# Values by seven products instead of eight, in turns with the keys

## The chip, the cores and the metric

The kernel runs on one core of a Trainium2 chip. The metric is the device time of one execution in microseconds; the time of a kernel is the median of several runs. All data are 32-bit floats.

## The reference

Sixteen batches of `x` (1024 nodes by 256 channels) go through two residual layers that share one 1024 x 1024 adjacency. The first layer forms queries by a graph product, keys and values by one weight matrix, and attends with four heads; the second is a two-step graph convolution. Cut to what matters here:

```python
c_adj = mean(x over channels)
A_s = symmetric likeness of c_adj[n], c_adj[m]
g = relu(einsum('bcn,bnm->bcm', x^T, adj * A_s) * para)     # queries
kv = x @ kv_w                                               # (B, N, 2C)
k, v = first C columns, last C columns, split into 4 heads of 64
attn = softmax(q k^T * scale)
x = layernorm(x + attn v)
h = relu(x @ w1_loop + adj @ (x @ w1_neigh) + b1)
h = relu(h @ w2_loop + adj @ (h @ w2_neigh) + b2)
x = layernorm(x + (x + h) * 0.5)
```

The change touches how `x @ kv_w` is computed and where one step of the softmax's denominators stands.

## The kernel before

One program handles the batches one after the other, with the order of every engine's work written out by hand (`manual_schedule`). In the loop over `b`, the attention of batch b is interleaved with the second layer of batches b-1 and b-2 and with the queries, keys and values of batch b+1.

**Attention** (`Attention`) runs over four units, a pair of heads by a half of the query nodes. `scores(u)` makes eight score tiles on TensorE (line 594), each exponentiated by ScalarE (L597) and summed by VectorE (L601, L603), then transposed (L605) and reduced (L607) into partial denominators. `outputs(u)` multiplies by the values (L614), and VectorE transposes the result (L618). `add(u)` folds the partial denominators with one small matmul (L626, tile `den_ps`), takes reciprocals (L630), multiplies (L632), adds to the residual (L634) and reduces (L635). Between units stand `gap0`, `gap1` and `gap2`; `gap0` holds the convolution's inner product (L712, tile `t_ps`) and then `att.add(0)`, `gap1` the joined adjacency products.

**Keys and values** (`KeysValues`) are made after the queries of the same batch. The transposed input `xT` and the key half of the weights are each cut into 2 x 2 blocks, and seven products of block sums replace eight (a Winograd form of Strassen's scheme): `sums` makes four combinations of `xT` on VectorE (L384 to L387), and four combinations of weight blocks are made once at the start on GpSimd (`sum_key_weights`, L135 to L138), stored in device memory and loaded again for each batch (`load`, L392). In `run`, products are accumulated onto PSUM that ScalarE has copied away in between (L411, L415, L420, L422 into `ksnap`), and the last additions are done by VectorE (L418, L426), GpSimd (L427) and, as a copy, ScalarE (L429). The values take the plain form: four groups (`value_group`) of four 128 x 128 by 128 x 256 matmuls each (L360), copied by ScalarE (L362). Groups stand between the key products.

In `run`, `between` is called before the first key addition and `later` before the last products. In the steady state they are `norm.variance` (a fold of squares, `sum_ps`, L250, then L324 on VectorE and a power on GpSimd, L326) and `q.scale` (L569 on VectorE, L570 on ScalarE). After `run` come `norm.scale` (L331) and `norm.spread` (transposes L219 and stores). The queries' end (L555 to L563) stands before `run`.

PSUM has three double banks (`big_psum`, tag "big") and two single ones (`bank_psum`). Row tiles of 128 x 1024 come from one pool of 25.

Of the kernel before, what the change touches and what calls it, by code (L numbers as in the profile page):

```python
# [10 lines left out]
F32 = mybir.dt.float32  # L11
# [7 lines left out]
def kernel(  # L19
# [31 lines left out]
    nc = tc.nc  # L51

    B, N, C = x.shape
    P = 128
    NT = N // P
    NC = C // P
# [3 lines left out]
    FB = 512  # L60
    NJ = N // FB
    TJ = FB // P
    EPS = 1e-5
# [19 lines left out]
    dram = ctx.enter_context(tc.tile_pool(name="dram", bufs=2, space=bass.MemoryType.DRAM))  # L83
# [15 lines left out]
    def row_tile(name):  # L99
        return work.tile([P, N], F32, tag="row", name=name, bufs=ROWS)  # L100
# [15 lines left out]
    for t0 in range(0, NT, 2):  # L116
        nc.sync.dma_start(out=x_first[:, t0:t0 + 2, :],
                          in_=x[0, t0 * P:(t0 + 2) * P, :].rearrange("(t p) c -> p t c", p=P))
    kvw_sb = const.tile([P, NC, 2 * C], F32, name="kvw_sb")
# [6 lines left out]
    b2_sb = const.tile([P, C], F32, name="b2_sb")  # L126


    key_sums = dram.tile([P, 4 * P], F32, tag="key_sums", name="key_sums", bufs=1)

    def sum_key_weights():
        a11, a21, a12, a22 = (kvw_sb[:, cc, ts(kb, P)] for cc in range(NC) for kb in range(NC))
        t = row_tile("key_sums")
        s1, s2, s3, s4 = (t[:, ts(n, P)] for n in range(4))
        nc.gpsimd.tensor_add(s1, a21, a22)  # L135
        nc.gpsimd.tensor_sub(s2, s1, a11)
        nc.gpsimd.tensor_sub(s3, a11, a21)
        nc.gpsimd.tensor_sub(s4, a12, s2)  # L138
        nc.sync.dma_start(out=key_sums, in_=t[:, 0:4 * P])

    def load_weights():
        nc.sync.dma_start(out=w1l_sb, in_=w1_loop.rearrange("(cc p) f -> p cc f", p=P))
# [101 lines left out]
        nc.scalar.copy(c_row, pc)  # L244
        return c_row

    def fold_sums(part, name):

        pm = bank_psum(f"{name}_ps")
        nc.tensor.matmul(pm[:, 0:NB], fold.rearrange("p a k -> p (a k)"), part[:, 0, :], start=True, stop=True)  # L250
        return pm[:, 0:NB]

# [45 lines left out]
    class BlockedNorm:  # L298
# [22 lines left out]

        def variance(self):
            self.rstd = small.tile([P, NB], F32, tag="rstd1", name=f"rstd1_{self.name}", bufs=2)
            nc.vector.tensor_scalar(self.rstd, fold_sums(self.part, f"sum2_{self.name}"), 1.0 / C, EPS,  # L324
                                    op0=ALU.mult, op1=ALU.add)
            nc.gpsimd.tensor_tensor(self.rstd, self.rstd, neg_half, ALU.pow)  # L326

# [27 lines left out]
    def value_group(b, v, xT, g, copy):  # L355
        per = FB // C
        pv = bank_psum(f"v_ps_{b}_{g}")
        for i in range(per):
            for cc in range(NC):
                nc.tensor.matmul(pv[:, ts(i, C)], xT[:, cc, ts(g * per + i, P)], kvw_sb[:, cc, C:2 * C],  # L360
                                 start=(cc == 0), stop=(cc == NC - 1))
        copy(v[:, g * per:(g + 1) * per, :], pv.rearrange("p (i c) -> p i c", c=C))  # L362
# [7 lines left out]
    class KeysValues:  # L370
# [17 lines left out]
            self.w = {1: w11, 2: w21, 3: w22, 4: t4, 5: t1, 6: t2, 7: t3}  # L388

        def load(self):  # L390
            t = row_tile(f"key_sums_{self.b}")
            nc.sync.dma_start(out=t[:, 0:4 * P], in_=key_sums)  # L392
            a11, a21, a12, a22 = (kvw_sb[:, cc, ts(kb, P)] for cc in range(NC) for kb in range(NC))
            self.a = {1: a11, 2: a12, 3: t[:, ts(3, P)], 4: a22, 5: t[:, ts(0, P)], 6: t[:, ts(1, P)], 7: t[:, ts(2, P)]}

        def run(self, between=lambda: None, later=lambda: None):
            b, xT = self.b, self.xT
            kT = work.tile([P, NC, N], F32, tag="kT", name=f"kT_{b}")
            v = work.tile([P, NT, C], F32, tag="v", name=f"v_{b}")
            first, third, second = (half_psum(f"k_ps_{b}_{i}") for i in range(3))  # L400
            s12, s34 = (row_tile(f"ksnap_{b}_{k}") for k in range(2))
            p1, u1, u3, p7 = s12[:, 0:FB], s12[:, FB:N], s34[:, 0:FB], s34[:, FB:N]

            def product(n, dst, again=False):
                nc.tensor.matmul(dst, self.a[n], self.w[n], start=not again, stop=True, skip_group_check=again)

            def group(g):
                value_group(b, v, xT, g, nc.scalar.copy)

            product(1, first)  # L410
            nc.scalar.copy(p1, first)  # L411
            product(2, third)
            group(0)
            product(6, first, again=True)
            nc.scalar.copy(u1, first)  # L415
            group(1)
            between()
            nc.vector.tensor_add(kT[:, 0, 0:FB], p1, third)  # L418
            product(5, first, again=True)
            nc.scalar.copy(u3, first)  # L420
            product(7, second)
            nc.scalar.copy(p7, second)  # L422
            group(2)
            later()
            product(4, second, again=True)
            nc.vector.tensor_add(kT[:, 1, 0:FB], u1, second)  # L426
            nc.gpsimd.tensor_add(kT[:, 1, FB:N], u3, p7)  # L427
            product(3, first, again=True)
            nc.scalar.copy(kT[:, 0, FB:N], first)  # L429
            group(3)  # L430
            return kT, v

    class Queries:
# [49 lines left out]
    class FastQueries(Queries):  # L483
# [16 lines left out]
        def block(self, i, j):  # L500
            return self.xb[:, j * TJ:(j + 1) * TJ, ts(i, P)]
# [70 lines left out]
    class Attention:  # L572
# [47 lines left out]
        def add(self, u):  # L620

            b, (pair, j) = self.b, UNITS[u]
            half = FB // S
            pd = bank_psum(f"den_ps_{b}_{u}")
            den = pd[:, 0:2 * half]
            nc.tensor.matmul(den, fold.rearrange("p a k -> p (a k)"), self.part.pop(u), start=True, stop=True)  # L626
            rden = self.rden[:, ts(u, half)]
            for s in range(2):
                rows = slice(s * HD, (s + 1) * HD)
                nc.vector.reciprocal(rden[rows, :], den[rows, ts(s, half)])  # L630
            o = by_node(self.o.pop(u))
            nc.vector.tensor_mul(o, o, rden.unsqueeze(2).to_broadcast([P, half, S]))  # L632
            dst = by_node(self.xB[pair][:, ts(j, FB)])
            nc.vector.tensor_add(dst, dst, o)  # L634
            nc.vector.tensor_reduce(self.sums[:, pair, ts(j, half)], dst, AX.X, ALU.add)  # L635
            if u == len(UNITS) - 1:
                join(self.sums)
                nc.vector.tensor_reduce(rden_min[:, b:b + 1], self.rden, AX.X, ALU.min)
                nc.vector.tensor_reduce(rden_max[:, b:b + 1], self.rden, AX.X, ALU.max)
# [293 lines left out]
    def run():  # L933
# [10 lines left out]
        xT, c_col = prepare_first(x_first)  # L944
        q = Queries(0, x_first)
        for t in range(NT):
            q.load(t)
        sum_key_weights()
        q.load_para()
        blocked = load_blocked(1, "1")  # L950
        tiles = {mt: adj_blocked(mt) for mt in (0, TJ, 1)}
# [6 lines left out]
        kT = keys(0, xT, first_weights)  # L958
        for t in (1, 2):
            q.likeness(t)  # L960
        v = values(0, xT, nc.vector.tensor_copy, 3)
# [29 lines left out]
        for b in range(B):  # L991
            more = b + 1 < B
            att = Attention(b, xB, qT, kT, v)
# [12 lines left out]
            def gap0():  # L1006
                row = means(q, xb, str(b + 1))
                c1.inner()
                att.add(0)
                if both:  # L1010
                    c2.load_x()
                    both.fetch(2, 3)
                    both.left(nc.gpsimd)
                row()
                ready["xT"] = channel_major(blocked, f"xT_{b + 1}")
# [34 lines left out]
            for u in range(len(UNITS)):  # L1050
                att.scores(u)
                if u == 1 and between:
                    kv = KeysValues(b + 1, ready["xT"])
                    kv.sums()
                if u == 3 and between:
                    for t in (2, TJ + 2, 3, TJ + 3):
                        q.load(t)
                    for t in (2, TJ + 2, 3, TJ + 3):
                        q.likeness(t)
                    q.right(1)  # L1060
                if u and (not between or u == 3 and not both):
# [167 lines left out]
```

## Time and profile before

| | |
|---|---|
| median of 3 runs | 2168.17 us (2167.69 to 2169.34) |
| profiled execution, whole time | 2168.41 us |
| its span, first to last instruction | 2166.5 us |
| mean granted TensorE clock | 0.998 |
| a value pass, v_ps, L360 | 512 passes, 120.9 us busy |
| a key product's pass, k_ps, L405 | 210 passes in all |
| inner product, t_ps, L712 | 512 passes, 61.3 us busy |
| load of the block sums, L392 | 256 KB, once for each of 15 batches |

Engines in the profile are PE (TensorE's matmuls), PEld (its weight loads), DVE (VectorE), ACT (ScalarE), POOL (GpSimd) and SP (the queue that issues the transfers). A group line gives line, engine, operation, tiles and shapes, then the count, the busy time, the mean length of one, and the idle time ahead of it with what ended it. A timeline line gives the start, the time covered, the engine and the merged instructions. An f32 matmul appears as two passes, each with its own weight load. Ends of matmuls are modelled and overlap the next start, so spacing is read from starts.

### The profile page before, as it was taken

How to read it: one execution, taken by the hardware profiler on the slowest of the kernel's cores; microseconds unless marked ns; L12 is line 12 of the kernel's file. 1: busy time of each engine (PE TensorE's matmuls, PEld its weight loads, DVE VectorE, ACT ScalarE, POOL GpSimd, SP SyncE). 2: the span in 40 equal slices, each digit the busy share in tenths (PEclk: the TensorE clock that was granted, in tenths of full speed). 3: DMA queues.
4: the chain of work that ended last, by engine and by line, in shares of the span. 5: the costliest groups of instructions: out<-in, count | busy, mean ns of one | idle time of the engine just before them, and what ended most of it. 6: DMA issues, size and time to landing. Idle time of an engine off the chain costs nothing.

```text
span 2166.5 us, 23100 instructions
## 1 busy us (share of the span) xinstructions
PE 2152.7 (99%) x8052; PEld 1024.6 (47%) x8052; DVE 1892.1 (87%) x2342; ACT 1033.5 (48%) x1359; POOL 368.5 (17%) x212
## 2 busy tenths in 40 slices
PE   9999999999999999999999999999999999999997
PEld 5344444444444444454545445454454444544354
DVE  5988988898998989998899888999989899898964
ACT  4745445545345554445443454445553445535412
POOL 1010130311303113030120302203022130211021
PEclk9999999999999999999999999999999999999999
DMA  9493664836557365573656537566374554744342
GB/s 229 121 139 117 144 153 105 144 126 119 154 122 160 107 121 156 127 168 89 115 171 121 158 88 116 171 122 156 97 117 160 122 156 115 122 148 82 118 136 99
DMA packets 611916, 286.49 MB, mean 132 GB/s; under 512 B 504784, under 2 KB 569168, under 8 KB 611792
## 3 DMA queue, kind: packets, MB, share of 16 engines
q1 hardware_dynamic: 611520, 284.41, 55.4%
q8 instruction: 65, 1.06, 0.2%
q14 instruction: 59, 0.48, 0.1%
q10 hardware_dynamic: 272, 0.52, 0.1%
HBM read 238.42 MB, written 46.46 MB: 131 GB/s over the span
## 4 chain that ended last, share of the span: by engine, by line


## 5 line engine op out<-in xcount | busy, mean ns | idle before, releaser
L597 ACT ACTIVATE pr<-s 128x1024 f32<-128x1024 f32 x512 | 476.1, 1054 | 176.1 <-PE s L594 176.1
L603 DVE TENSOR_TENSOR acc<-acc,pr 128x1024 f32<-128x1024 f32 x384 | 494.2, 1287 | 41.1 <-DVE acc L603 1.0
L594 PE MATMUL s<-qT,kT 64*128 64x512 f32 x2048 | 456.8, 596 | 0.0
L614 PE MATMUL av<-pr,v 128*64 128x512 f32 x2048 | 453.6, 595 | 0.0
L594 PEld LDWEIGHTS s<-qT,kT 64*128 64x128 f32 x2048 | 191.6, 186 | 234.9 <-ACT pr L597 111.3
L614 PEld LDWEIGHTS av<-pr,v 128*64 128x64 f32 x2048 | 141.3, 137 | 299.3 <-issue 284.9
L326 POOL TENSOR_TENSOR rstd<-rstd,neg_half 128x32 f32<-128x32 f32 x16 | 87.1, 5442 | 1113.1 <-DVE rstd L324 1113.1
L459 ACT ACTIVATE wg<-c_row,c_col 128x1024 f32<-128x1024 f32 x128 | 147.0, 1148 | 69.2 <-DVE accB L605 50.5
L465 DVE SCALAR_TENSOR_TENSOR wg<-wg,adj 128x1024 f32<-128x1024 f32 x128 | 150.0, 1210 | 12.8 <-ACT wg L460 11.9
L892 PE MATMUL hu_ps<-adj,R 128*128 128x512 f32 x360 | 158.3, 596 | 0.0
L460 ACT ACTIVATE wg<-wg 128x1024 f32<-128x1024 f32 x128 | 135.4, 1058 | 4.1
L314 ACT ACTIVATE sq<-xB_a 128x1024 f32<-128x1024 f32 x32 | 33.8, 1057 | 197.0 <-DVE xB_a L309 195.7
L360 PE MATMUL v_ps<-kvw_sb,xT 128*128 128x256 f32 x512 | 120.9, 379 | 0.1
L546 PE MATMUL g_ps<-wg,S 128*128 128x512 f32 x224 | 116.7, 603 | 0.0
L360 PEld LDWEIGHTS v_ps<-kvw_sb,xT 128*128 128x128 f32 x512 | 97.2, 190 | 40.1 <-issue 22.5
L546 PE MATMUL g_ps<-T,S 128*128 128x512 f32 x224 | 114.4, 592 | 0.0
L546 PE MATMUL g_ps<-wg,x 128*128 128x512 f32 x224 | 109.0, 599 | 0.0
L892 PE MATMUL hu_ps<-adjT,t 128*128 128x512 f32 x240 | 105.7, 592 | 0.0
L892 PEld LDWEIGHTS hu_ps<-adj,R 128*128 128x128 f32 x360 | 67.3, 190 | 78.9 <-issue 76.0
L601 DVE TENSOR_TENSOR acc<-pr,pr 128x1024 f32<-128x1024 f32 x64 | 76.8, 1201 | 20.5 <-ACT pr L597 20.5
L605 DVE STREAM_TRANSPOSE accB<-acc 128x1024 f32<-128x1024 f32 x64 | 79.7, 1245 | 3.3
L908 ACT COPY snap<-hu_ps 128x512 f32<-128x512 f32 x15 | 8.8, 585 | 150.3 <-PE hu_ps L892 146.2
(189 smaller groups left out, 2923.0 us busy)
## 6 DMA issues: line engine op xcount, KB each, us to landing
adj<-in_adj_dram SPq DMA_DIRECT2D x128, 512.0 KB, 4.7
adj<-adjT SPq DMA_DIRECT2D x120, 512.0 KB, 10.2
para<-in_L_gnn_para_dram SPq DMA_DIRECT2D x32, 512.0 KB, 3.4
xB_a<-in_x_dram SPq DMA_DIRECT2D x128, 128.0 KB, 4.3
x1d<-xB_a SPq DMA_DIRECT2D x128, 128.0 KB, 3.4
x<-x1d SPq DMA_DIRECT2D x16, 1024.0 KB, 16.5
xB<-in_x_dram SPq DMA_DIRECT2D x120, 128.0 KB, 4.3
x<-in_x_dram SPq DMA_DIRECT2D x15, 1024.0 KB, 7.9
```

What stands on the lines that cost most here:

```text
L326: nc.gpsimd.tensor_tensor(self.rstd, self.rstd, neg_half, ALU.pow)
L360: nc.tensor.matmul(pv[:, ts(i, C)], xT[:, cc, ts(g * per + i, P)], kvw_sb[:, cc, C:2 * C], start=(cc == 0), stop=(cc == NC - 1))
L459: nc.scalar.activation(wg, self.c_row, AF.Abs, bias=self.c_col[:, t:t + 1], scale=-1.0)
L460: nc.scalar.activation(wg, wg, AF.Tanh, scale=-0.5)
L465: nc.vector.scalar_tensor_tensor(wg, wg, 1.0, self.adj.pop(t), op0=ALU.add, op1=ALU.mult)
L546: nc.tensor.matmul(self.p[n], x_n[:, k, :], w_n, start=(k == 0), stop=(k == TJ - 1))
L594: nc.tensor.matmul(ps[:, ts(s, FB)], self.kT[rows, pair, ts(mt, P)], self.qT[rows, pair, ts(j, FB)], start=True, stop=True)
L597: nc.scalar.activation(pr, ps, AF.Exp)
L603: nc.vector.tensor_add(acc, acc, pr)
L605: nc.vector.transpose(accB, acc)
L614: nc.tensor.matmul(pav[s * HD:(s + 1) * HD, :], self.v[:, mt, pair * P + s * HD:pair * P + (s + 1) * HD], self.pr[mt][:, ts(s, FB)], start ...
L892: nc.tensor.matmul(dst, self.x[n][:, k, :], half_adj[w][:, k, :] if w else of_rows(rows, k), start=(start and k == 0), stop=(k == TJ - 1), ...
```

## The change

The values get the same seven-product form as the keys. The weight sums are made for both halves (eight GpSimd operations, one 512 KB tile stored, and loaded once per batch). `run` alternates: each key product of 512 columns is followed by the value product of the same number, which is four 128 x 128 blocks by 128 columns. ScalarE copies the value accumulators into `vsnap`; three value blocks and two key blocks, and the key block that was GpSimd's, are final additions on VectorE, and one key and one value block are ScalarE copies. The first two additions now stand before `between`. The fold in `variance` takes its PSUM from the "big" tag instead of "bank". `att.add(0)` moves out of `gap0` to a place after `scores(1)` and ahead of the block sums of the next batch and of `outputs(1)`. The last batch (15) and the first (0) keep their order for `att.add`; the keys and values of batch 0 keep the plain form.

```diff
-    def sum_key_weights():
-        a11, a21, a12, a22 = (kvw_sb[:, cc, ts(kb, P)] for cc in range(NC) for kb in range(NC))
-        t = row_tile("key_sums")
...
+    kv_sums = dram.tile([P, N], F32, tag="kv_sums", name="kv_sums", bufs=1)
+
+    def sum_kv_weights():
+        t = row_tile("kv_sums")
+        for k in range(2):
+            a11, a21, a12, a22 = (kvw_sb[:, cc, ts(2 * k + kb, P)] for cc in range(NC) for kb in range(NC))
+            s1, s2, s3, s4 = (t[:, ts(4 * k + n, P)] for n in range(4))
+            nc.gpsimd.tensor_add(s1, a21, a22)
+            nc.gpsimd.tensor_sub(s2, s1, a11)
+            nc.gpsimd.tensor_sub(s3, a11, a21)
+            nc.gpsimd.tensor_sub(s4, a12, s2)
+        nc.sync.dma_start(out=kv_sums, in_=t)
...
-    def fold_sums(part, name):
+    def fold_sums(part, name, psum_tile=bank_psum):
-        pm = bank_psum(f"{name}_ps")
+        pm = psum_tile(f"{name}_ps")
...
-            nc.vector.tensor_scalar(self.rstd, fold_sums(self.part, f"sum2_{self.name}"), 1.0 / C, EPS,
+            nc.vector.tensor_scalar(self.rstd, fold_sums(self.part, f"sum2_{self.name}", half_psum), 1.0 / C, EPS,
...
+        def key(self, n, dst, again=False):
+            nc.tensor.matmul(dst, self.a[0][n], self.w[n], start=not again, stop=True, skip_group_check=again)
+
+        def value(self, n, dst, again=False):
+            for t in range(TJ):
+                nc.tensor.matmul(dst[:, ts(t, P)], self.w[n][:, ts(t, P)], self.a[1][n],
+                                 start=not again and t == 0, stop=True, skip_group_check=again or t > 0)
...
-            product(1, first)
-            nc.scalar.copy(p1, first)
-            product(2, third)
-            group(0)
-            product(6, first, again=True)
-            nc.scalar.copy(u1, first)
-            group(1)
+            k_first, v_first = half_psum(f"k_ps_{b}_0"), bank_psum(f"v_ps_{b}_0")
+            self.key(1, k_first)
+            copy(p1, k_first)
+            self.value(1, v_first)
+            copy(y1, v_first)
+            k_next, v_next = half_psum(f"k_ps_{b}_1"), bank_psum(f"v_ps_{b}_1")
+            self.key(2, k_next)
+            add(kT[:, 0, 0:FB], p1, k_next)
+            self.value(2, v_next)
+            add(block(0, 0), tiles(y1), tiles(v_next))
+            self.key(6, k_first, again=True)
+            copy(u1, k_first)
+            self.value(6, v_first, again=True)
+            copy(z1, v_first)
+            self.key(5, k_first, again=True)
+            copy(u3, k_first)
+            self.value(5, v_first, again=True)
+            copy(z3, v_first)
             between()
-            nc.vector.tensor_add(kT[:, 0, 0:FB], p1, third)
-            product(5, first, again=True)
-            nc.scalar.copy(u3, first)
-            product(7, second)
-            nc.scalar.copy(p7, second)
-            group(2)
+            k_next, v_next = half_psum(f"k_ps_{b}_2"), bank_psum(f"v_ps_{b}_2")
+            self.key(7, k_next)
+            copy(p7, k_next)
+            self.value(7, v_next)
+            copy(y7, v_next)
             later()
-            product(4, second, again=True)
-            nc.vector.tensor_add(kT[:, 1, 0:FB], u1, second)
-            nc.gpsimd.tensor_add(kT[:, 1, FB:N], u3, p7)
-            product(3, first, again=True)
-            nc.scalar.copy(kT[:, 0, FB:N], first)
-            group(3)
+            add(kT[:, 1, FB:N], u3, p7)
+            add(block(1, 1), tiles(z3), tiles(y7))
+            self.key(3, k_first, again=True)
+            copy(kT[:, 0, FB:N], k_first)
+            self.value(3, v_first, again=True)
+            copy(block(0, 1), tiles(v_first))
+            self.key(4, k_next, again=True)
+            add(kT[:, 1, 0:FB], u1, k_next)
+            self.value(4, v_next, again=True)
+            add(block(1, 0), tiles(z1), tiles(v_next))
             return kT, v
...
                 c1.inner()
-                att.add(0)
                 if both:
...
                 if u == 1 and between:
+                    att.add(0)
                     kv = KeysValues(b + 1, ready["xT"])
                     kv.sums()
```

More of the change, by code (lines that the diff above doesn't have):

```diff
@@ L126 @@
     b2_sb = const.tile([P, C], F32, name="b2_sb")
-    key_sums = dram.tile([P, 4 * P], F32, tag="key_sums", name="key_sums", bufs=1)
-    def sum_key_weights():
-        a11, a21, a12, a22 = (kvw_sb[:, cc, ts(kb, P)] for cc in range(NC) for kb in range(NC))
-        t = row_tile("key_sums")
[L134 to L139, printed above, removed]
+    kv_sums = dram.tile([P, N], F32, tag="kv_sums", name="kv_sums", bufs=1)
[9 more added lines that the diff above has]
+        nc.sync.dma_start(out=kv_sums, in_=t)
     def load_weights():
@@ L390, in load @@
         def load(self):
[L391 to L394, printed above, removed]
+            t = row_tile(f"kv_sums_{self.b}")
+            nc.sync.dma_start(out=t, in_=kv_sums)
+            self.a = []
+            for k in range(2):
+                a11, a21, a12, a22 = (kvw_sb[:, cc, ts(2 * k + kb, P)] for cc in range(NC) for kb in range(NC))
+                s1, s2, s3, s4 = (t[:, ts(4 * k + n, P)] for n in range(4))
+                self.a.append({1: a11, 2: a12, 3: s4, 4: a22, 5: s1, 6: s2, 7: s3})
@@ L396, in run @@
+        def key(self, n, dst, again=False):
[4 more added lines that the diff above has]
+                                 start=not again and t == 0, stop=True, skip_group_check=again or t > 0)
         def run(self, between=lambda: None, later=lambda: None):
-            b, xT = self.b, self.xT
+            b = self.b
@@ L398, in run @@
             kT = work.tile([P, NC, N], F32, tag="kT", name=f"kT_{b}")
             v = work.tile([P, NT, C], F32, tag="v", name=f"v_{b}")
[L400 to L405, printed above, removed]
@@ L407, in group @@
-            def group(g):
-                value_group(b, v, xT, g, nc.scalar.copy)
-            product(1, first)
-            nc.scalar.copy(p1, first)
-            product(2, third)
-            group(0)
-            product(6, first, again=True)
-            nc.scalar.copy(u1, first)
-            group(1)
-            between()
-            nc.vector.tensor_add(kT[:, 0, 0:FB], p1, third)
-            product(5, first, again=True)
-            nc.scalar.copy(u3, first)
-            product(7, second)
@@ L422, in run, with copies @@
-            nc.scalar.copy(p7, second)
-            group(2)
-            later()
-            product(4, second, again=True)
-            nc.vector.tensor_add(kT[:, 1, 0:FB], u1, second)
-            nc.gpsimd.tensor_add(kT[:, 1, FB:N], u3, p7)
-            product(3, first, again=True)
-            nc.scalar.copy(kT[:, 0, FB:N], first)
-            group(3)
+            def copies(name):
+                s12, s34 = (row_tile(f"{name}snap_{b}_{k}") for k in range(2))
+                return s12[:, 0:FB], s12[:, FB:N], s34[:, 0:FB], s34[:, FB:N]
@@ new lines, in block, with tiles @@
+            def block(i, j):
+                return v[:, ts(j, TJ), ts(i, P)]
+            def tiles(t):
+                return t.rearrange("p (t c) -> p t c", c=P)
+            p1, u1, u3, p7 = copies("k")
+            y1, z1, z3, y7 = copies("v")
+            copy, add = nc.scalar.copy, nc.vector.tensor_add
+            k_first, v_first = half_psum(f"k_ps_{b}_0"), bank_psum(f"v_ps_{b}_0")
[3 more added lines that the diff above has]
+            copy(y1, v_first)
@@ L947, in run @@
             q.load(t)
-        sum_key_weights()
+        sum_kv_weights()
         q.load_para()
```

## The prediction

> **What bounds the kernel now.** I read the page's shares first, then the groups, then the timeline of TensorE in one batch in the middle of the run, and last the work of VectorE in the same batch.
>
> ```profile
> PE 2152.7 (99%) x8052; PEld 1024.6 (47%) x8052; DVE 1892.1 (87%) x2342; ACT 1033.5 (48%) x1359; POOL 368.5 (17%) x212
> ```
>
> A busy PE alone proves little: the Trainium skill (Perfetto Trace Analysis, "Identifying the Most-Contended Engine") calls matmul occupancy a poor measure, since pipelined matmuls overlap. So I look at when matmuls start.
>
> ```profile
> 1052.28 2.23 PE L405 MATMUL k_ps<-xT,kvw_sb 128*128 128x512 f32 x4
> 1054.34 1.89 PE L360 MATMUL v_ps<-kvw_sb,xT 128*128 128x256 f32 x8
> 1056.06 1.02 PE L405 MATMUL k_ps<-K,key_sums 128*128 128x512 f32 x2
> 1056.92 1.89 PE L360 MATMUL v_ps<-kvw_sb,xT 128*128 128x256 f32 x8
> 1058.65 0.30 PE L250 MATMUL sum_ps<-sq_part,fold 128*128 128x32 f32 x2
> 1058.79 1.96 PE L405 MATMUL k_ps<-K,key_sums 128*128 128x512 f32 x4
> 1060.59 1.89 PE L360 MATMUL v_ps<-kvw_sb,xT 128*128 128x256 f32 x8
> 1062.32 1.02 PE L405 MATMUL k_ps<-K,kvw_sb 128*128 128x512 f32 x2
> 1063.17 1.02 PE L405 MATMUL k_ps<-xT,key_sums 128*128 128x512 f32 x2
> 1064.03 1.89 PE L360 MATMUL v_ps<-kvw_sb,xT 128*128 128x256 f32 x8
> 1065.85 0.70 PE L594 MATMUL s<-qT,kT 64*128 64x512 f32 x2
> ```
>
> This is the timeline of TensorE over one keys-and-values stage; the first column is the start, the second the time covered. An f32 matmul shows as two passes, so x2 is one product. Differences of starts: a key product takes 0.86 us (1056.06 to 1056.92), a value group of 8 passes 1.72 to 1.73 (1054.34 to 1056.06), so 0.216 a pass. No hole follows any group: the table by stage gives 133.13 us of busy PE in a batch's 133.20, at a granted clock of 1.00, and key stages of successive batches begin 133.2 us apart. **TensorE sets the end**, and what shortens its stream shortens the run, as long as nobody makes it wait. The stage lasts 13.57 us: 6.02 for 14 key passes of 0.43, 6.91 for values, 0.14 for the fold, and the rest waits. The first group shows one: 4 key passes take 2.06 us, not 1.72. Single passes put the third at 1053.38, 0.67 behind the second (L558 on VectorE had to empty its PSUM first), so 0.34 is lost here.
>
> **What the Trainium skill says.** TensorE: Matmul & The Clock Gate, "Back-to-back issue gap", says the spacing of a stream is set by the weight load and the matmul together; "LDWEIGHTS" there gives columns/1.2 ns, 107 ns for 128. That matters: the new value products move 128 columns per weight load, the old ones 256. The trace has the very form, in the graph convolution's inner product:
>
> ```profile
> 1079.94 3.84 PE L712 MATMUL t_ps<-w1n_sb,x1T 128*128 128x128 f32 x32
> 1083.61 0.31 PE L626 MATMUL den_ps<-den_part,fold 128*128 128x32 f32 x2
> 1083.85 1.56 PE L594 MATMUL s<-qT,kT 64*128 64x512 f32 x6
> ```
>
> 32 passes in 3.67 us, the first 0.1 longer after a wait: 0.112 a pass. It agrees with the page's 107, and I use 0.112. SBUF — State Buffer, "SBUF: two separate sides", says that GpSimd and a VectorE operation with two SBUF inputs lock each other out. The trace agrees:
>
> ```profile
> 1083.96 0.52 DVE L630 RECIPROCAL rden<-den_ps 64x16 f32<-64x16 f32 x2 [1.29 <-PE den_ps L626]
> ...
> 1085.24 1.65 DVE L634 TENSOR_TENSOR xB_a<-xB_a,o 128x512 f32<-128x512 f32 x1
> ```
>
> L634 takes 1.65 us while POOL's L883 runs, and 0.69 elsewhere; L331 takes 2.28 beside POOL's key addition (L427), and its second half 1.21 without it.
>
> **Part by part, for one batch.**
> - Values: 32 passes of 0.216 (6.91) become 7 x 4 x 2 = 56 of 0.112 (6.26): **-0.65**. Bounds: 0.107 (-0.92) and the group's whole 61.3/512 = 0.120 (-0.19).
> - The turns: a value product of 0.89 now stands between keys 1 and 2. L558 ends at 1053.32 and key 2 comes at 1052.28 + 0.86 + 0.89 = 1054.03, so the wait of L558 goes: **-0.34**. Value 2 needs the bank that L559 empties by 1054.11; it comes at 1054.89.
> - New handoffs. Key 6, value 6, key 5, value 5 add onto PSUM that ScalarE must have copied. Key 6 ends at 1056.65; its copy starts 0.63 after its last pass began (1056.49 to 1057.12 now) and takes 0.585, so it ends at 1057.44, and key 5 is due at 1057.54. For value 6 the same gives 1058.33 against 1058.40. All else on PE queues behind these two. A product released late pays 0.1 for its first pass (0.697 against 0.592 us). I take **+0.12**; bounds 0, and 0.5 if each copy comes 0.2 later.
> - Key 7 and value 7 need VectorE's first two additions. Its sums end with L563 at 1058.50, the additions (0.6 apart) at 1059.1 and 1059.8; PE wants these buffers at 1059.7 and 1060.5. No cost.
> - Den: `att.add(0)` moves its fold from behind the inner product (t_ps to s: 0.35 with it, 0.21 without, as v_ps to s is 0.31 for a 0.216 pass: 0.14) to between scores and outputs of unit 1. Batch 15 has that place now:
>
> ```profile
> 2032.81 1.45 PE L594 MATMUL s<-qT,kT 64*128 64x512 f32 x6
> 2034.20 0.41 PE L626 MATMUL den_ps<-den_part,fold 128*128 128x32 f32 x2
> 2034.53 1.94 PE L614 MATMUL av<-pr,v 128*64 128x512 f32 x8
> ```
>
> The last score pass there starts at 2033.68, outputs at 2034.53: 0.86, where 0.53 is the usual step (scores to outputs, 1090.39 to 1090.92): 0.33. Moved: **+0.19**.
> - VectorE gains four additions of 0.6 (three value blocks, one key block taken from POOL) and loses 1.07 of L331's contention: +1.4. Its waits in the stage (0.48, 1.33, 0.67) absorb part. `variance` now stands behind two additions, so POOL's 5.44 us power ends near 1065.4, not 1064.70, and L331 starts near 1065.5 with scores due at 1065.0. VectorE enters unit 0 about 0.8 us later against PE. Then the 1.29 of L630 goes, since the quotients (0.52 + 0.69 + 0.69 + 0.69) run behind unit 1's sums. There POOL's L507 and L508 (3.35 us) contend with L632 and L634 instead of L385 and L386 (1.75 each against 0.69 now). VectorE still has waits of 1.11 (L741), 1.07 (L601), 0.97 (L787) later in the batch, so it is back in step before the query products. Cost on PE: 0.
> - ScalarE: five copies of values for four, +0.6 of 48% busy; the two L570 come before the last copies, as now. 0.
> - SP: the load of sums doubles to 512 KB; para's loads of that size land in 3.4 us, and product 6 comes some 15 us after the issue. The store at the start waits for eight POOL operations of 0.455 instead of four (+1.8 us, to about 8.9; the store is issued at 8.74 now). Behind it SP's queue holds para, the blocked loads and the adjacency; VectorE has 2.87 us idle before L479. 0, at most +0.3 once.
>
> Sum: -0.65 - 0.34 + 0.12 + 0.19 = **-0.68** a batch, for 14 batches -9.5. The stage of batch 1 has neither the wait nor the moved fold: -0.53. Together -10.1. The profiled execution took 2168.41 us (span 2166.5, 1.9 around it), the median is 2168.17. So 2158.3 against the former, **2158.0** as a median.
>
> **The rivals.**
> - *The handoffs eat it.* If ScalarE's copies come late by 0.5 us (copies queue behind each other, up to two per product pair), key 5 and value 5 both wait that long: +1.0 for my 0.12, and the batch is +0.2 longer: 2171; half of it gives 2164. For it: 0.1 us of spare. Against: ScalarE idles between its copies in this stage now.
> - *Weight loads at every turn* (slower). A key pass (0.43) hides the load for the next value pass; the reverse load has only 0.112 to hide in, and a LDWEIGHTS record lasts 190 ns. If each of the 14 switches costs 0.1, that is +1.4 for a gain of 0.68: +0.7 a batch, **2179**. It decides from 0.05 a switch. Against: den_ps starts 0.11 after the last t_ps pass, and k_ps follows v_ps without a gap.
> - *VectorE becomes the bound.* It leaves PE alone until its lag exceeds the 3.15 us of those three waits; then scores of unit 3 wait for L787. I find 0.8, at most 3 with all contention against it. Each us beyond costs 14: one us gives 2172.
> - *It doesn't do what it says:* fewer columns may leave TensorE idle where it was busy, with the same batch period, since the next score tile must wait for `kT` or a copy anyway: 2168. Against: the last score-side input, L570, is done about 2 us before the scores.
>
> **Numbers.** My forecast 0.74 (2154 to 2164, from the bounds of pass and handoff), handoffs 0.10, weight loads 0.07, VectorE 0.05, nothing 0.04. The measurement tells 0.2% from no change, 4.3 us: faster below 2163.8. That gives 0.78 faster, 0.11 within, 0.11 slower. The range 2154 to 2165 leaves out the slower cases and a little below.
>
> **Right or wrong.** In the profile after: v_ps with 128 columns, x56 a batch, spacing near 0.112; no third-pass wait in k_ps; ScalarE's copies starting without a queue; key stage to first score 12.8 us instead of 13.57; den_ps between s and av, 0.33 each; the multiplication of L331 at 1.2 instead of 2.28 us; batch period 132.5. A spacing above 0.124 for the value passes, or PE gaps before keys 5 and values 5 above 0.4 each, would make it wrong.

## The result and the profile after

| | before | after |
|---|---|---|
| median | 2168.03 us (2167.69 to 2169.34, 6 runs) | 2160.56 us (2160.30 to 2161.69, 6 runs) |
| profiled execution, its span | 2168.41, 2166.5 | 2160.70, 2158.9 |
| batch period in the steady state | 133.20 | 132.82 |
| first key product to first score | 13.23 (13.57 to 13.67 in three batches) | 12.66 |

The ratio is 0.9966, with a 95% interval of 0.9956 to 0.9977. The change makes the kernel faster by 7.5 us (0.3%); 10.1 had been forecast. A batch period is the time from the first key product of one batch to that of the next; a usual batch is one of the steady state in which TensorE has no wait that the other batches don't have.

The page of the kernel after has this row of busy times and instructions by engine:

```profile
PE 2145.5 (99%) x8412; PEld 1030.9 (48%) x8412; DVE 1906.0 (88%) x2402; ACT 1040.9 (48%) x1374; POOL 361.7 (17%) x201
```

TensorE still sets the end, with 360 matmul passes more (15 stages of 56 for 32) and 7.2 us less busy time. Its timeline over a keys-and-values stage in the middle of the run (start, time covered, line, output and inputs, passes):

```profile
1048.97 1.02 PE L401 MATMUL k_ps<-xT,kvw_sb 128*128 128x512 f32 x2
1049.83 1.05 PE L405 MATMUL v_ps<-kvw_sb,xT 128*128 128x128 f32 x8
1050.72 1.02 PE L401 MATMUL k_ps<-xT,kvw_sb 128*128 128x512 f32 x2
...
1053.33 1.05 PE L405 MATMUL v_ps<-kv_sums,K 128*128 128x128 f32 x8
1054.22 1.07 PE L401 MATMUL k_ps<-K,kv_sums 128*128 128x512 f32 x2
1055.13 1.09 PE L405 MATMUL v_ps<-kv_sums,K 128*128 128x128 f32 x8
1056.06 0.31 PE L251 MATMUL sum_ps<-sq_part,fold 128*128 128x32 f32 x2
1056.20 1.10 PE L401 MATMUL k_ps<-K,kv_sums 128*128 128x512 f32 x2
...
1060.64 1.05 PE L405 MATMUL v_ps<-kvw_sb,K 128*128 128x128 f32 x8
1061.63 1.56 PE L624 MATMUL s<-qT,kT 64*128 64x512 f32 x6
...
1075.71 3.84 PE L742 MATMUL t_ps<-w1n_sb,x1T 128*128 128x128 f32 x32
1079.48 7.14 PE L624 MATMUL s<-qT,kT 64*128 64x512 f32 x32
1086.55 0.41 PE L656 MATMUL den_ps<-den_part,fold 128*128 128x32 f32 x2
1086.89 1.51 PE L644 MATMUL av<-pr,v 128*64 128x512 f32 x6
```

Read differences of starts. A value product takes 0.89 (1049.83 to 1050.72): 8 passes of 0.111. The key product behind it takes 0.86, as without a turn. Only key 5 (1054.22 to 1055.13: 0.91) and value 5 (0.93) wait a little for ScalarE's copies (the new handoffs of the prediction). The moved fold stands between scores and outputs and takes 0.34.

By starts over the whole run, the value passes take 9.6 us less (0.64 in each of 15 stages, with the small wait at value 5 counted in), and the key passes 0.1 less: the waits at key 2, of which the next section tells, are gone, and the waits at key 5 take most of that back. The fold at its new place costs 2.3 more (den_ps 1.3, t_ps 1.0), and the first products of all take 0.1 more. The sum is -7.25, and the last product does begin 7.25 earlier (2155.13 and 2147.89). The other 0.35 by which the span is shorter lies behind the last product, and no run shows that it belongs to the change.

VectorE over the same stage and the end of unit 1 (in brackets: its idle time before the instruction, and what ended it):

```profile
1056.40 0.19 DVE L325 TENSOR_SCALAR rstd<-sum_ps 128x32 f32<-128x32 f32 x1 [0.36 <-PE sum_ps L251]
1056.51 2.41 DVE L599 TENSOR_TENSOR qT<-qT,para 128x1024 f32<-128x1024 f32 x2
...
1063.05 2.36 DVE L332 TENSOR_TENSOR xB_a<-xB_a,rstd 128x1024 f32<-128x1024 f32 x2 [0.63 <-POOL rstd L327]
...
1096.46 0.51 DVE L660 RECIPROCAL rden<-den_ps 64x16 f32<-64x16 f32 x2
1097.00 1.43 DVE L662 TENSOR_TENSOR o<-o,rden 128x512 f32<-128x512 f32 x1
1098.46 1.64 DVE L664 TENSOR_TENSOR xB_a<-xB_a,o 128x512 f32<-128x512 f32 x1
```

L332 is x2 in 2.36 us, so 1.2 each, where its first half took 2.28 beside GpSimd's key addition. The quotients (L660 on) no longer wait for den_ps; they run beside GpSimd's L537 and L538 and take longer there. Nothing of this reaches TensorE. ScalarE's copies start without a queue: 0.31 us of idle or more stand before each of the stage's first eight.

### The profile page after: what moved, and what is told of

It reads as the page before. It is cut to its first block, busy times and chain, and to the rows that moved or that the text cites. A ratio compares the mean times of both kernels' runs of the same rounds, so it can differ in the third digit from the quotient of the medians.

```text
span 2158.9 us, 23875 instructions
## 1 busy us (share of the span) xinstructions
PE 2145.5 (99%) x8412; PEld 1030.9 (48%) x8412; DVE 1906.0 (88%) x2402; ACT 1040.9 (48%) x1374; POOL 361.7 (17%) x201
## 3 DMA queue, kind: packets, MB, share of 16 engines
q8 instruction: 68, 1.11, 0.2%
## 4 chain that ended last, share of the span: by engine, by line
## 5 line engine op out<-in xcount | busy, mean ns | idle before, releaser
L633 DVE TENSOR_TENSOR acc<-acc,pr 128x1024 f32<-128x1024 f32 x384 | 498.9, 1299 | 41.1 <-DVE acc L633 1.0
L327 POOL TENSOR_TENSOR rstd<-rstd,neg_half 128x32 f32<-128x32 f32 x16 | 99.8, 6238 | 1129.8 <-DVE rstd L325 615.6
L631 DVE TENSOR_TENSOR acc<-pr,pr 128x1024 f32<-128x1024 f32 x64 | 83.2, 1300 | 23.8 <-ACT pr L627 23.8
L635 DVE STREAM_TRANSPOSE accB<-acc 128x1024 f32<-128x1024 f32 x64 | 79.7, 1245 | 3.5 <-DVE acc L633 0.5
L637 DVE TENSOR_REDUCE den_part<-accB 128x32 f32<-128x1024 f32 x64 | 78.1, 1220 | 2.2
L810 PE MATMUL h_ps<-w2n_sb,uT 128*128 128x256 f32 x240 | 72.7, 385 | 0.0
```

The source lines that it names most:

```text
L631: nc.vector.tensor_add(acc, self.pr[0], pr)
L633: nc.vector.tensor_add(acc, acc, pr)
L635: nc.vector.transpose(accB, acc)
```

## The wait at key 2: one batch taken for all

The forecast counted 0.34 us in each of 14 batches for a wait at key 2, read from one batch. Here is the kernel before one batch later, first TensorE, then VectorE:

```profile
1185.82 1.88 PE L405 MATMUL k_ps<-xT,kvw_sb 128*128 128x512 f32 x4
1187.54 1.89 PE L360 MATMUL v_ps<-kvw_sb,xT 128*128 128x256 f32 x8
```

```profile
1185.84 0.68 DVE L558 TENSOR_TENSOR U<-U,g_ps 128x512 f32<-128x512 f32 x1
```

Four key passes take 1.72: no wait. L558 ends 0.70 after key 1 begins; key 2's first pass is due at 0.86. In the batch that the prediction shows, L558 ended 1.04 after key 1, and key 2 followed it by 0.06. Of the 14 stages of batches 2 to 15, three have the wait: those that begin at 252.18 (four passes in 2.16), 1052.28 (2.06) and 1319.02 (2.09). The other eleven have 1.72. It comes to (2.16 + 2.06 + 2.09) - 3 x 1.72 = 1.15 us in the run, not 4.8.

In the batch that the prediction shows, VectorE was late because of something that had happened one unit earlier (VectorE, kernel before):

```profile
1023.88 1.23 DVE L603 TENSOR_TENSOR acc<-acc,pr 128x1024 f32<-128x1024 f32 x1
1025.57 2.56 DVE L603 TENSOR_TENSOR acc<-acc,pr 128x1024 f32<-128x1024 f32 x2 [0.46 <-DVE acc L603]
```

An idle of 0.46 us stands between two additions that follow each other within about 0.1 elsewhere. It names only the addition before it, not a late input: the last exponential that these additions read (L597) had ended at 1022.22. From here to L558, everything on VectorE is 0.36 later than in the batch before, and the delay reaches key 2 by way of ScalarE:

```profile
1048.74 2.19 ACT L314 ACTIVATE sq<-xB_a 128x1024 f32<-128x1024 f32 x2 [12.73 <-DVE xB_a L309]
1050.84 0.57 ACT L555 COPY P<-g_ps 128x512 f32<-128x512 f32 x1
```

```profile
1051.44 0.69 DVE L556 TENSOR_TENSOR U<-P,g_ps 128x512 f32<-128x512 f32 x1 [1.66 <-ACT P L555]
```

ScalarE's squares (L314) wait for VectorE's L309, the copy L555 stands behind them in ScalarE's order, and L556 to L558 wait for that copy. So VectorE's 1.66 us of idle before L556 absorb nothing. The stage at 1319.02 has such an idle too, 0.47 at 1287.02. The one at 252.18 has none, and the kernel with only the fold moved has a wait of the same size in the same batch; its cause was not traced.

## Experiments

Each ratio is to the kernel before, run on the same chip; its medians there were 2168.05 (in the first eight runs) and 2167.88 (in the last three).

### Only the value products taken back

```diff
 # kernel after; keys in their new order
-self.value(1, v_first) ... self.value(4, v_next, again=True)   # seven products, four additions
+group(0), group(1), group(2), group(3)                         # value_group, as before
```

> The changed kernel with the values in the plain form again (four groups of 256 columns, ScalarE copies) between the key products, which keep the changed order and VectorE's last addition. Theory (the shorter value stream is the gain): 15 x 0.66 comes back, 15 x 0.05 to 0.08 of handoffs goes: 2160.6 + 9.9 - 1.0 = 2169.5 us, above the kernel before by the moved fold. Rival (the order of the key products and the freed GpSimd carry the gain): 2163 us or less.

2169.40 us (2168.57 to 2169.78), ratio 1.0005 (0.9997 to 1.0014). TensorE's timeline in this kernel:

```profile
1054.01 1.89 PE L361 MATMUL v_ps<-kvw_sb,xT 128*128 128x256 f32 x8
1055.74 1.02 PE L401 MATMUL k_ps<-xT,kvw_sb 128*128 128x512 f32 x2
```

A group is 1.73 again, v_ps gains exactly the 9.6 us it had lost, and the stage is 13.23 as in the kernel before. The rest of the change costs 1.4 us by itself, so the seven products are the whole gain and pay for that too. By starts (1.5 us in the profiled execution), that rest is 2.3 for the fold and 0.3 for the first products, less 1.1 for the keys. Nothing is left for the other parts of the change, which were not tried alone. The 1.1 is the wait at key 2: key 2 comes 1.73 + 0.86 after key 1 begins here, and the wait for the addition that was L558 appears in no batch.

### Only the fold moved

```diff
 # kernel before: gap0
-                att.add(0)
 # Attention loop, u == 1 and between
+                    att.add(0)
```

> The kernel before with one edit of the change alone: the first unit's fold and quotients moved to between the second unit's scores and outputs. Theory: +0.19 us x 14 batches on TensorE, 2170.6 us. Rival (the move hides VectorE's work and gains by itself, or is free): 2168.0 us or less.

2170.05 us (2169.53 to 2170.60), ratio 1.0009 (1.0001 to 1.0018). TensorE:

```profile
1080.64 3.84 PE L712 MATMUL t_ps<-w1n_sb,x1T 128*128 128x128 f32 x32
1084.41 7.14 PE L594 MATMUL s<-qT,kT 64*128 64x512 f32 x32
1091.47 0.41 PE L626 MATMUL den_ps<-den_part,fold 128*128 128x32 f32 x2
1091.81 1.51 PE L614 MATMUL av<-pr,v 128*64 128x512 f32 x6
```

t_ps to scores is 3.77 (3.67 with the fold behind it), the fold 0.34 (0.24 there), and the batch period 133.39 for 133.20: the predicted 0.19. The move by itself costs time. Of the 0.19 x 14 = 2.7 it gives 0.8 back. In batch 2 of the kernel before, the fold behind the inner product waits 0.45 for VectorE's L607 (t_ps takes 4.02 there instead of 3.67, den_ps 0.34 instead of 0.24), and here it doesn't. And two batches of this kernel have the wait at key 2 (four passes in 2.16 and 2.06), not three.

### The fold taken back out of the change

```diff
 # kernel after: gap0
+                att.add(0)
 # u == 1 and between
-                    att.add(0)
```

> The changed kernel with the first unit's fold and quotients back behind the inner product; everything else stays changed. Theory (the moved fold costs TensorE about 0.19 us a batch: 0.34 between scores and outputs against 0.15 behind the inner product): 2160.6 - 14 x 0.1 to 0.19 = 2158.0 to 2159.2 us. The range is open below 0.19 since VectorE's partial denominator (L637) ends within 0.1 us of the place where the fold would start. Rival (the move is needed: the fold now waits for that denominator, or VectorE gets late): 2160.6 us or more, with a gap before den_ps behind t_ps.

2161.51 us (2160.93 to 2163.40), ratio 0.9971 (0.9959 to 0.9982): the 0.19 is not won back. A usual batch is shorter (132.70, by 0.12; den_ps takes 0.31 here instead of 0.24), but two batches wait. TensorE, VectorE and GpSimd in one of them:

```profile
1209.57 3.84 PE L742 MATMUL t_ps<-w1n_sb,x1T 128*128 128x128 f32 x32
1214.34 0.41 PE L656 MATMUL den_ps<-den_part,fold 128*128 128x32 f32 x2 [0.93 <-DVE den_part L637]
```

```profile
1202.77 8.98 DVE L633 TENSOR_TENSOR acc<-acc,pr 128x1024 f32<-128x1024 f32 x6
...
1213.06 1.22 DVE L637 TENSOR_REDUCE den_part<-accB 128x32 f32<-128x1024 f32 x1
```

```profile
1209.40 1.26 POOL L912 TENSOR_TENSOR R<-h 128x512 f32<-128x512 f32 x1 [1.32 <-DVE acc L633]
```

Six additions took 8.98, where six of the same kind take 7.87 without GpSimd: GpSimd's L912 held one up by 1.11. From it to den_part everything on VectorE is back to back, and the fold starts 1.09 late (4.76 for t_ps instead of 3.67). In batch 2 t_ps takes 5.47; there VectorE has also to finish the adjacency (L201 to L204, 2.5 us) before L332. So the move buys room: it costs 0.12 to 0.19 in every batch and removes waits of 1 to 2 us in some. In this kernel, with the seven products, that is about even: 1 us in favour of moving, on medians whose ranges overlap.

### The fold moved further, into the next gap

```diff
 # kernel after: gap1, instead of u == 1 and between
+                att.add(0)
 # o of unit 0 kept in a row tile until then
```

> The changed kernel with the first unit's fold and quotients at the start of gap1, behind the second unit's outputs (the first unit's transposed outputs then live in a row tile). Theory (what costs is the change of shape on TensorE between scores and outputs, 0.34 with the fold and less where the shapes change anyway): the fold costs 0.14 to 0.24 there, so 0.1 to 0.2 us x 14 goes: 2158 to 2159 us, and no wait for the denominators. Rival (the fold is as dear anywhere): 2160.6 us.

2162.34 us (2161.18 to 2164.24), ratio 0.9974 (0.9964 to 0.9984). The fold costs 0.24 there and a usual batch is 132.70, but two batches wait for VectorE at the *second* unit's fold. TensorE and VectorE in one of them:

```profile
1768.36 0.41 PE L656 MATMUL den_ps<-den_part,fold 128*128 128x32 f32 x2 [1.56 <-DVE o L648]
```

```profile
1762.58 1.76 DVE L386 TENSOR_TENSOR K<-xT 128x512 f32<-128x512 f32 x1
...
1767.60 0.70 DVE L648 STREAM_TRANSPOSE o<-av 128x512 f32<-128x512 f32 x1
```

The four block sums that make `K` come first on VectorE, and three of them take 1.7 instead of 0.68 while GpSimd's L535 to L538 run. The expected 2158 to 2159 us were missed: a cheaper place for the fold on TensorE puts a wait for VectorE in its stead.

### One addition more on VectorE, before and after

```diff
 # either kernel, end of the queries: an addition done twice
             add(qT[:, 0, h0], p1, p[2])
+            add(qT[:, 0, h0], p1, p[2])
```

> The kernel before with one VectorE addition of the queries' end (L557) done twice, which writes the same values and makes L558 0.6 us later in 14 batches. Theory (before, key product 2 has no slack against L558: it waits whenever VectorE is late, and in the profile only 3 batches were): every batch now waits, 0.5 to 0.6 us x 14 = 7 to 8 us: 2175 to 2176 us. Rival (there is slack, and the waits of those batches are something else): 2168 us.

> The changed kernel with the same addition done twice. Theory (with a value product between keys 1 and 2, key 2 comes 0.89 us later and takes the delay): 2160.6 us, within 1. Rival (the delay moves on to key 7 and value 7 or to the scores): up to +0.6 x 14, 2169 us.

Before: 2178.36 us (2178.25 to 2178.55), ratio 1.0048 (1.0034 to 1.0061). After: 2162.45 (2161.75 to 2162.62), ratio 0.9974 (0.9963 to 0.9984). The same addition costs 10.3 us before (7 to 8 had been expected) and 1.9 after (at most 1 had been). TensorE in the kernel before with it (L559 is the former L558):

```profile
1191.35 1.02 PE L405 MATMUL k_ps<-xT,kvw_sb 128*128 128x512 f32 x2
1192.83 1.13 PE L405 MATMUL k_ps<-xT,kvw_sb 128*128 128x512 f32 x2 [0.46 <-DVE U L559]
```

Now every batch from 2 to 15 has the wait: key 2 comes 1.48 after key 1 instead of 0.86, and the four passes take 2.43 to 2.88 instead of 1.72: 0.7 in a usual batch, and more where the kernel before, or this one, is late for another reason. Without the addition, L558 ended 0.70 after key 1 begins and key 2 followed L558 by 0.06 where it waited, so of the 0.86 about 0.1 us was to spare. That decides in which batches there is a wait. In the kernel after, keys 1 and 2 keep 1.75 between them in a usual batch; what is left of the late addition there is 0.06 at the fold of squares and key 7, and 0.4 in two batches. These two runs show that the value product between the keys does what the prediction said of it; it was worth only 1.15 us because the wait was rare.

### The remaining handoffs

```diff
 # kernel after: variance's fold ahead of key 5, in the free half of the second key tile
+            between(k_two[:, FB:N])
             self.key(5, k_first, again=True)
...
-            between()
```

> The changed kernel with the fold of the squares (sum_ps) ahead of key 5 instead of behind value 5, in the free half of key 2's PSUM tile. Theory: the fold covers the handoffs of key 5 and value 5 (0.05 and 0.03 us a batch), so 14 x 0.08 = 1.1 us goes: 2159.5 us. Rival (those 0.08 are not waits for ScalarE's copies): no change, 2160.6 us.

2178.30 us (2178.15 to 2178.89), ratio 1.0048 (1.0034 to 1.0062), a miss. TensorE:

```profile
1063.61 0.41 PE L251 MATMUL k_ps<-sq_part,fold 128*128 128x32 f32 x2 [1.12 <-DVE kT L434]
```

The fold waits for VectorE's addition L434, which reads the other half of the same tile, and all of TensorE stands behind it: 1.28 in a usual batch. The addition and the fold use different halves, so no value needs this wait; it follows from the order in which the program records them on one tile. The next kernel records VectorE's first two additions behind the fold:

```diff
+            between(k_two[:, FB:N])
+            add(kT[:, 0, 0:FB], p1, k2_next)
+            add(block(0, 0), tiles(y1), tiles(v2_next))
             self.key(5, k_first, again=True)
```

> As e5_spare_half, but the first two additions on VectorE are recorded behind the fold of the squares, so that the fold doesn't wait for the key addition that reads the same tile. Theory: the 1.3 us wait per batch of e5_spare_half goes, and the fold covers the handoffs of key 5 and value 5 (0.05 and 0.03): 2160.6 - 1.1 = 2159.5 us. Rival (the 0.08 are no waits for copies): 2160.6 us; if the wait has another cause it stays at 2178 us.

2159.35 us (2159.10 to 2159.66), ratio 0.9960 (0.9946 to 0.9973). TensorE:

```profile
1053.79 0.31 PE L251 MATMUL k_ps<-sq_part,fold 128*128 128x32 f32 x2
1053.93 1.10 PE L401 MATMUL k_ps<-K,kv_sums 128*128 128x512 f32 x2
1054.88 1.05 PE L405 MATMUL v_ps<-kv_sums,K 128*128 128x128 f32 x8
1055.77 1.02 PE L401 MATMUL k_ps<-K,kv_sums 128*128 128x512 f32 x2
```

Key 7 (1055.77) and value 5 before it (0.89) no longer wait; the 0.1 that follows the fold falls on key 5 (0.95), where a handoff wait stood anyway. The stage is 12.58, shorter by 0.08: that is the whole price of the two handoffs, for which the prediction took 0.12. It has the lowest median of all the kernels here, 1.2 us under the kernel after, with ranges that do not touch; by starts, its last product begins 1.1 earlier. VectorE is earlier too: L332 begins 0.72 behind the first score (1061.83 and 1061.11) instead of 1.42.

### The key addition given back to GpSimd

```diff
-            add(kT[:, 1, FB:N], u3, p7)
+            nc.gpsimd.tensor_add(kT[:, 1, FB:N], u3, p7)
```

> The changed kernel, with the addition of the key block kT[1, FB:N] given back to GpSimd, as it was before the change. The prediction costed the taking over of this addition by VectorE at nothing, and the end of the contention at L332 (1.225 us now, 2.28 before) as a gain for VectorE alone. If VectorE's work is covered: L332 back at about 2.3 us, the batch period 132.82 as in the changed kernel, total 2160.6 within 1. Rival: VectorE's lag reaches TensorE when L332 is a microsecond longer, so that scores or a fold wait in some batches: 0.4 to 1.7 us for each such batch, as seen with the fold put back, 2162 to 2166.

2159.81 us (2159.80 to 2159.99), ratio 0.9963 (0.9949 to 0.9976). VectorE:

```profile
1063.05 3.42 DVE L332 TENSOR_TENSOR xB_a<-xB_a,rstd 128x1024 f32<-128x1024 f32 x2 [0.63 <-POOL rstd L327]
```

L332's two halves take 1.06 more, the contention is back, and TensorE's starts add up to the same time as in the kernel after (+0.04 us, batch period 132.82). So VectorE's extra addition and the end of the contention are covered, as the prediction costed them. The 0.9 by which this execution's span is shorter lies behind the last product (begun at 2147.91, 2147.89 in the kernel after), so it is not an effect of the edit that I can show.

### Both fold edits joined with the handoff edit

Two kernels, each with the handoff edit of above and one of the two other places for the fold:

> The changed kernel with two edits at once: the first unit's fold back behind the graph convolution's inner product, and the fold of the squared differences ahead of key 5, in the free half of the second key tile, with VectorE's first two additions recorded behind it. Alone the first gave 2161.5 (0.12 less in a usual batch, but two batches in which the fold waited for VectorE), the second 2159.35. Theory: the second brings VectorE into unit 0 about a microsecond earlier, which is the slack that the fold lacked, so the waits go and only the 0.12 of each usual batch is left: 2159.35 - 14 x 0.12 = 2157.7. Rival: the waits come from single GpSimd operations that start beside the last L633 of the unit, wherever VectorE stands; then two batches still pay, and it is about 2160.3.

> The changed kernel with two edits at once: the first unit's fold and quotients at the start of the stretch before unit 1's scores' successor (the second gap of the attention), and the fold of the squared differences ahead of key 5 with VectorE's first two additions behind it. Alone the first gave 2162.3 (0.12 less in a usual batch, two batches in which the second unit's fold waited 1.7 us or more), the second 2159.35. If the earlier VectorE ends those waits: 2157.7. If they come from the bank that VectorE's quotients free, whatever its start: 2161 to 2162.

The first took 2159.45 us (2159.07 to 2161.38), ratio 0.9960 (0.9947 to 0.9974); the second 2159.98 (2159.83 to 2161.86), ratio 0.9965 (0.9952 to 0.9979). Usual batches are the shortest of all, 132.54 and 132.62, but single batches still wait for VectorE. In the profiled execution of the first, the slowest of its five, they are three: t_ps takes 5.47 in batch 2 (where VectorE has the adjacency to finish, and the scores that follow take 1.69 more besides), and 4.10 and 4.05 in two others. In one of these a 0.46 idle and a slowed addition stand together (VectorE; line numbers are two higher here, so L635 is the former L633):

```profile
414.07 2.03 DVE L635 TENSOR_TENSOR acc<-acc,pr 128x1024 f32<-128x1024 f32 x1 [0.46 <-DVE acc L635]
```

In the second kernel one batch waits 2.2 us at the second unit's fold. Neither reaches the 2157.7 of the theory, nor quite the time of its rival (2160.3, and 2161 to 2162). A fold that is cheaper on TensorE pays in single batches about what it gains in the usual ones, and the fold's place in the change is as good as any tried.

## Why the prediction was right in direction and too large in size

Point by point, by its own steps:

- **Values, -0.65 a batch.** Measured -0.67 (6.91 to 6.24, handoffs apart), 15 times. The price of a 128-column pass, taken from t_ps in the same profile, held to 0.001 us. The bounds around it (-0.19 to -0.92) were not needed.
- **The wait at key 2, -0.34 a batch: the step that failed.** The mechanism was right: the value product between the keys takes the wait away, and the kernels with one addition more show it. The size was wrong, since it was multiplied by 14 from one batch, and three have it: -1.15 in all for -4.8. The lines had a warning. The stage shown begins at 1052.28 and the next at 1185.82, which is 133.54 apart; the prediction took 133.2, the period of a batch without the wait, and subtracted the wait from it. Without that term its sum is -0.65 + 0.12 + 0.19 = -0.34, a period of 132.86, and 132.82 was measured. A list of all stages by their length (13.23, or 13.57 and more) would have shown it before.
- **Handoffs, +0.12.** Measured 0.05 at key 5 and 0.03 at value 5: 0.08.
- **The moved fold, +0.19.** Measured 0.19 alone and with the rest of the change.
- **VectorE, ScalarE, SP and GpSimd, 0.** Held. L332 begins 1.42 behind the first score (0.5 was worked out), mostly since GpSimd's power took 6.35 us instead of 5.44; VectorE still is in step by the next query products, and neither a microsecond more in L332 nor one addition more made TensorE wait by more than 0.1 in a usual batch.

With the measured sizes the sum of a usual batch is -0.67 + 0.08 + 0.19 = -0.40, and the periods say -0.38. The run as a whole is -0.38 x 14 - 0.58 (the first stage) - 1.15 (the waits at key 2) - 0.45 (the wait of the fold in batch 2, which the prediction didn't have) + 0.10 (a wait at key 1 in batch 2) + 0.14 (the first products) = -7.3, beside the 7.25 by which the last product begins earlier. So the forecast had 3.6 us too much for the multiplied wait (4.8 for 1.15), and the other terms came out 0.8 better. More than half of that 0.8 is the finer sizes of values and handoffs; the 0.45 in batch 2 is luck. The stage of 12.8 us that the prediction names is 12.7 by its own terms; 12.66 was measured.

Of the rivals, the weight loads fall by the timeline: a key product behind a value product takes 0.86, as elsewhere, and value products 0.89, where 0.05 a switch was the point from which it would have decided. Handoffs that eat the gain fall by the 0.08. VectorE as the bound falls for the change as it stands, but it is near: with the fold at its former place it held TensorE up by 1 to 2 us in single batches. That nothing changes falls with the result. Against that rival the prediction said that L570 is done about 2 us before the scores; it ended at 1065.00, 0.85 before them. In the kernel after, VectorE's last addition to kT (L458) ends at 1061.53, 0.1 before the first score, but the scores don't wait for it: the last value product takes 0.98 up to them, 0.09 more than the others, and the last value group took 0.09 more than the others before the change too.

## What to carry to other kernels

A wait seen in one pass through a loop is a sample: list the same stretch of every pass, and multiply only what all of them have. A chain with 0.1 us to spare waits when something else has been late, and a piece of work put in between takes that away; it is worth the number of times that it happens. For a matmul of another shape the nearest row of the same shape elsewhere in the profile gave its price to a hundredth of a microsecond, and moving a small step off a busy engine's path can pay for itself although it costs time in every pass, if it stood where another engine had no room; here it came out about even.

## What was unexpected of the hardware

- GpSimd's power on a tile of 128 x 32 takes 5.44 us in all 16 batches of the kernel before, and 6.35 in most after. The trace's view of that line (least, median and largest duration in ns, first and last start), for the kernel after and then for the kernel with the fold first:

```profile
L327 POOL TENSOR_TENSOR rstd<-rstd,neg_half x16: 5437/6348/6367, 133.2 to 2068.9; 128x32 f32<-128x32 f32 x16
```

```profile
L327 POOL TENSOR_TENSOR rstd<-rstd,neg_half x16: 5436/5437/5460, 133.2 to 2067.8; 128x32 f32<-128x32 f32 x16
```

  In the kernel after it starts 0.16 after L599, a multiplication by VectorE with both inputs in SBUF (1056.67 and 1056.51); with the fold first it starts beside an addition that reads PSUM, and takes 5.44 again. The Trainium skill (SBUF — State Buffer, "SBUF: two separate sides") says that whichever of two such operations starts first holds the shared port for its whole length. For the one that starts second, both measurements agree: the 0.91 is near the 1.04 that is left of L599's first half, and the 1.11 of the slowed addition near the 1.26 of the GpSimd operation beside it. But a power that starts first doesn't hold VectorE for its whole length. In the kernel before, both multiplications L569, with both inputs in SBUF, run inside it at their usual 1.22 each (GpSimd, then VectorE):

```profile
1059.26 5.44 POOL L326 TENSOR_TENSOR rstd<-rstd,neg_half 128x32 f32<-128x32 f32 x1 [72.51 <-DVE rstd L324]
```

```profile
1059.69 2.35 DVE L569 TENSOR_TENSOR qT<-qT,para 128x1024 f32<-128x1024 f32 x2
```

  So for this operation the measurement departs from the page; which part of its 5.44 us holds the port is not shown.
- The same fold of two passes costs TensorE 0.14 between the inner product and scores (3.67 and 0.24 with it, 3.77 without), 0.22 between values and keys (0.14, and 0.08 on key 7), and 0.34 between scores and outputs. It is the place, not the fold, that makes the price.
- VectorE has idles of 0.46 us between two dependent additions, at most a few in a run and mostly at different times in different runs, which no other instruction in the trace explains. The traces of the 13 kernels have 35 of them behind the first 100 us. Behind 25, a transfer on one of the two queues that the page lists as `instruction` (q8 and q14, 124 transfers in the kernel before) begins 0.6 to 1.7 us after the idle ends; behind the same additions without an idle, that is so for 408 of 4944. That points to instruction fetching, but it is a coincidence in time, and no run tested it.
